# Separate due times for the first two batches' own work in a two-layer graph network kernel

## The chip, the cores and the metric

One core of one Trainium2 chip. The time is the device time of one execution, in microseconds (us); lower is better. TensorE is PE in the profile, VectorE is DVE, ScalarE is ACT, GpSimd is POOL, SyncE is SP.

## The reference

16 batches of 1024 nodes with 256 features, and an adjacency matrix of 1024 x 1024 for each. Layer 0 is masked attention with 8 heads of 32, a projection of (normed heads, features) and a residual; layer 1 is two graph attentions one after the other, a residual, and a feed-forward of width 1024. Cut to what matters:

```python
# layer 0
q, k, v = heads(x @ Wq), heads(x @ Wk), heads(x @ Wv)
e = einsum('whqd,whkd->whqk', q, k)
e = where(e >= 0, e, ALPHA * e)
attn = softmax(where(adj[:, None] > 0, e, NEG), axis=-1)
h = merge_heads(einsum('whqk,whkd->whqd', attn, v))
out = layernorm(concatenate([layernorm(h), x], -1) @ Wffn.T)
x = out + x
# layer 1
def gat(h, W, a):
    Wh = h @ W
    e = leaky_relu(Wh @ a[:256] + swap(Wh @ a[256:]), ALPHA)
    return softmax(where(adj > 0, e, NEG), axis=1) @ Wh
h = layernorm(x + gat(gat(x, W1, a1), W2, a2))
out = layernorm(h + relu(h @ w_ff1 + b_ff1) @ w_ff2 + b_ff2)
```

## The kernel before

The program is written once for all batches, and the order of its instructions is worked out when it is built. Each piece of work is a Python generator (a "thread") that tells a planner, `Order`, what it is about to do: which engine and for how long (`on`), that it waits for an event, takes or gives a buffer, or starts another thread with an aim, a due time on the planner's clock. `Order.run` asks of every active thread when its next operation could start. Among those that can start within `WINDOW` (300 ns) of the earliest, it takes the one with the lowest aim:

```python
first = min(c[0][0] for c in could)
(t, engine, cost), th = min((c for c in could if c[0][0] <= first + self.WINDOW),
                            key=lambda c: (c[1]["aim"], c[1]["no"]))
```

The thread then emits the instruction. So the planner's clock and costs give only an order: on the chip every engine, and every queue that issues DMAs, goes through its own list in that order and waits for what it needs. DVE and POOL operations that are marked `shared` exclude each other in the plan (`port`); where the chosen one is of the one engine and a shared one of the other could begin at least 100 ns sooner, that one goes first. A free choice between two engines (`evacuate`, `weights` of batch 0) is made by the planner too.

Each batch has these stages, all under the names of the code:
- `project(b)`: `x_pair` loads x (256 KB a DMA, issued by ACT) and transposes it on PE (L347); `make_mask` and `mask_part` load the adjacency (DMA issued by ACT, L393), turn it into -1 and 0 in fp8 on DVE (L399), transpose it on PE (L409) and copy it (L413); `project_qk` and `qk_part` make q and k (L461), split them in two halves that sum to the fp32 value (L464, L466) and store both halves to DRAM on SP's queue (L470); `project_v` and `v_part` make v (L490).
- `load_stacks`: reads the halves of a head's q and k back on SP's queue (L545) into one of two pairs of buffers.
- `all_scores`: per head, 8 tiles of 128 x 1024 scores on PE (L578); `weights`: leaky ReLU on ACT and DVE (L596, L594, L598), exp on ACT (L601), the mask's product on POOL (L605).
- `all_values`: weights times v on PE (L627), `after_head`: transposed (L653) and divided (L658, L660).
- `rest(b)`, begun when the last values of b are planned: `rows_pair` (norms, L729 and L732, x1, L761), the first graph attention (`first_half` L797 to L801; `attend`, eight tiles of DVE work L814 and L817; `second_rows` L851), the second (`attend` again; `normed_pair` L876), and `feed_forward` (`hidden` L916, then L944), four pairs of row tiles each.

The projections of batch b + 1 are started when the scores of batch b begin, and `rest(b)` goes on beside the tiles of batch b + 1 and, with its feed-forward, of b + 2. `begin[b]` is the planner's time when b's scores begin. `SLOT` is 253 us of the planner's clock, and every aim is a share of it, from the table `AIM`: for `project(b + 1)` counted from `begin[b]`, for `rest(b)` from its own start, for `feed_forward` from the end of its pair's norm. A name ending in `_step` is what is added from one piece to the next. Batch 0 is projected with a start of -SLOT, so that its aims are the same shares less one.

Tiles are due at equal steps after `begin[b]`, and may be planned at most `lead` steps ahead of their due time. The pace of a batch is a share of SLOT:

```python
def pace(b):
    return PACE * {0: AIM["fast0"], 1: AIM["fast1"], B - 1: AIM["fast15"]}.get(b, 1.0)
...
                    due = t0 + (h * NT + t) / 2 * pace(b)
                    yield aim(due, AIM["lead"] * PACE)
```

Of the kernel before, what the change touches and what calls it, by code (L numbers as in the profile page):

```python
# [185 lines left out]
def wait(event):  # L186
    return "wait", event
# [14 lines left out]
def start(thread, aim):  # L202
    return "start", (thread, aim)
# [21 lines left out]
def unshifted_path(  # L225
# [9 lines left out]
    B, N, D = x.shape  # L235
# [14 lines left out]
    SLOT = 253e3  # L250
    PACE = SLOT / (H * NT // 2)


    AIM = dict(mask0=0.6, x=0.818, x_step=0, mask=0.747, mask_step=0.0264, qk0=0.614, qk1=0.898, qk_step=0.0231, v0=0.832,
               v1=0.974, v_step=0.0591, rows=-0.244, rows_step=0.0408, first0=0.12, first1=0.252,
               graph0=-0.009, graph1=0.21, graph_step=0, second=0.355, second_step=0.0335, normed=0.78,
               normed_step=0.026, ff_wait=(None, 0, 1, 0), ff=(0.532, -0.011, 0.487, 0.497), ff_step=0.0386,
               fast0=0.4, fast1=0.85, fast15=0.832, lead=3.15)

    const = ctx.enter_context(tc.tile_pool(name="const", bufs=1))  # L260
    sb = ctx.enter_context(tc.tile_pool(name="sb", bufs=1))
# [3 lines left out]
    bufs = dict(misc=3, scores=2, acc=1, p=5, stacks=2, stage=2, adj=2, adjb=2, pair=18,  # L265
                xT=2, v=2, mask=2, hn=1, w8=2, big=1, job=1)
    work = Order(**bufs)

    def misc(dtype=FT):
        return psum.tile([P, HALF], dtype, tag="misc", name="ps_m", bufs=bufs["misc"])  # L270
# [148 lines left out]
    def make_mask(b, t0):  # L419
        yield take("mask")  # L420
        masks[b] = buf([P, NT * N], "mask", "mask", F8)
        parts = [(t, (kh,)) for kh in range(NH) for t in range(NT)] if b == 0 else [(t, (0, 1)) for t in range(NT)]
        for n, (t, halves) in enumerate(parts):
            yield start(mask_part(b, t, halves), t0 + (AIM["mask" if b else "mask0"] + AIM["mask_step"] * n) * SLOT)

    def mask_of(b, t):

# [49 lines left out]
    def project_qk(b, g, t0):  # L477
        scratch[b, g] = dram.tile([2, P, 2, N], FT, name="qk_halves")
        for o in range(2):
            for nh in range(NH):  # L480
                yield start(qk_part(b, g, o, nh), t0 + (2 * o + nh) * AIM["qk_step"] * SLOT)

    def v_part(b, g, u):
        yield wait(("xT", b, u))
# [18 lines left out]
    def project_v(b, g, t0):  # L503
        yield take("v")
        v = buf([P, NT, G * VW + 31], "v", "v")
        vs[b, g] = v
        yield on(POOL=500)
        nc.gpsimd.memset(v[:, :, G * VW:], 0.0)
        nc.gpsimd.memset(v[:, :, :G * VW].rearrange("p t (h c) -> p t h c", c=VW)[:, :, :, DH:], -1.0)
        for u in range(NP):  # L510
            yield start(v_part(b, g, u), t0 + AIM["v_step"] * u * SLOT)

    def project(b, t0):
        yield take("xT")
        xTs[b] = buf([P, DC, N], "xT", "xT")
        for u in range(NP):
            yield start(x_pair(b, u), t0 + (AIM["x"] + AIM["x_step"] * u if b else 0.0) * SLOT)
        yield start(make_mask(b, t0), t0 + (0.5 if b else 0.0) * SLOT)
        for g in range(H // G):
            yield start(project_qk(b, g, t0 + AIM[("qk0", "qk1")[g]] * SLOT), t0)  # L520
            yield start(project_v(b, g, t0 + AIM[("v0", "v1")[g]] * SLOT), t0 + (0.8, 1.0)[g] * SLOT)

    def load_stacks():

# [300 lines left out]
    def attention(b, s, rows, at):  # L825

        yield take("w8")
        firsts[b, s] = buf([P, 2, N], "w8", "first")
        for nh in range(NH):
            yield start(first_half(b, s, nh), at(AIM[("first0", "first1")[s]]))  # L830
        for t in range(NT):
            yield wait(("row", b, s, t))
        second = small.tile([P, NT], FT, name="second", bufs=2)
        yield on(ACT=220)
        nc.scalar.activation(second, scores_of(b, s)[:, :, 1], AF.Exp, scale=1.0 - ALPHA)
        sums = small.tile([P, NT], FT, name="sums", bufs=2)
        yield take("big")
        big = buf([P, NT, N], "big", "att")
        yield fire(("graph", b, s))
        for j in range(NT):  # L840
            yield start(attend(b, s, big, rows, j, second, sums), at(AIM[("graph0", "graph1")[s]] + AIM["graph_step"] * j))
        for j in range(NT):
            yield wait(("att", b, s, j))
        yield give("w8")
        return big
# [19 lines left out]
    def normed_pair(b, u, big, y2):  # L865

        tiles = (2 * u, 2 * u + 1)
        yield wait(("x1", b, u))
        x1 = x1s.pop((b, u))
        yield take("misc")  # L870
        pa = misc()
        for i, t in enumerate(tiles):
            for half in range(2):
                yield on(PE=1720)
                for j in range(half * NT // 2, (half + 1) * NT // 2):
                    nc.tensor.matmul(pa[:, i * D:(i + 1) * D], big[:, j, t * P:(t + 1) * P], y2[:, j, :D],  # L876
                                     start=(j == 0), stop=False)
            yield on(PE=430)
            as_rows(pa, i, x1, i)
        yield fire(("weighed", b, u))  # L880
        yield give("pair")
        y, rows, srcs = yield from taken_out(pa, "y")
        mv, rs = yield from stats(srcs)
        yield from normalized(rows, srcs, mv, rs)
        yield take("pair")
        rT = buf([P, DC, 2 * P], "pair", "rT")
        yield take("misc")
        pt = misc()
        yield on(PE=450)
        transposes(pt, rows)  # L890
        yield give("pair")
        for dc in range(DC):
            yield from by_columns(rT[:, dc, :], pt[:, dc * 2 * P:(dc + 1) * 2 * P], k["gl1c"][:, dc:dc + 1],
                                  k["bl1c"][:, dc:dc + 1])
        yield give("misc")

        if b + 1 < B and AIM["ff_wait"][u] is not None:
            yield wait(("graph", b + 1, AIM["ff_wait"][u]))
        yield start(feed_forward(b, u, rT), work.now + (AIM["ff"][u] if b + 1 < B else 0.04 * u) * SLOT)

    def as_rows(pa, i, srcT, t):

# [25 lines left out]
        yield fire(done + (hp,))  # L928

    def feed_forward(b, u, rT):  # L930
        due = work.now + (AIM["ff"][u] if b + 1 < B else 0.04 * u) * SLOT
        yield take("job")
        hid = {}
        for hp in range(HC // 2):
            yield start(hidden(hid, rT, hp, ("hid", b, u)), due + AIM["ff_step"] * hp * SLOT)
        for hp in range(HC // 2):
            yield wait(("hid", b, u, hp))
        yield take("misc")
        pa = misc()
        for i in range(2):  # L940
            for half in range(2):
                yield on(PE=1720)
                for hc in range(half * HC // 2, (half + 1) * HC // 2):
                    nc.tensor.matmul(pa[:, i * D:(i + 1) * D], hid[hc // 2][:, hc % 2, i * P:(i + 1) * P], wf2[:, hc, :],  # L944
                                     start=(hc == 0), stop=False)
            yield on(PE=430)
            as_rows(pa, i, rT, i)
        for _ in range(HC // 2 + 1):
            yield give("pair")
        yield give("job")  # L950
        y, rows, srcs = yield from taken_out(pa, "z")
        mv, rs = yield from stats(srcs)
        for i, (row, src) in enumerate(zip(rows, srcs)):
            yield on(DVE=490, shared=True)
            nc.vector.scalar_tensor_tensor(row, src, mv[:, i, 0:1], k["gl2"], op0=OP.subtract, op1=OP.mult)
            yield on(DVE=490, shared=True)
            nc.vector.scalar_tensor_tensor(row, row, rs[:, i:i + 1], k["bl2"], op0=OP.mult, op1=OP.add)
        yield load()
        nc.sync.dma_start(out[b, 2 * u * P:2 * (u + 1) * P, :].rearrange("(p i) d -> p i d", p=P), y)
        yield give("pair")  # L960
        yield fire(("out", b, u))
# [6 lines left out]
    def rest(b):  # L968
# [3 lines left out]
        def at(share):  # L972
            return t0 + share * SLOT
# [6 lines left out]
        for q in range(NH):  # L980
            yield start(head_stats(b, q), at(0))
        for u in range(NP):
            yield start(rows_pair(b, u), at(AIM["rows"] + AIM["rows_step"] * u))
        for u in range(NP):
            yield wait(("hn used", b, u))
        yield give("hn")
# [2 lines left out]
        yield take("w8")  # L989
        y2 = buf([P, NT, YW], "w8", "y2")  # L990
        for i in range(NT):
            yield start(second_rows(b, big, y1, y2, i), at(AIM["second"] + AIM["second_step"] * i))
        for i in range(NT):
            yield wait(("row", b, 1, i))
        yield give("big")
        yield give("w8")
        for u in range(2):
            yield start(fetch_x1(b, u), at(AIM["normed"]))
        big = yield from attention(b, 1, y2, at)
        yield give("mask")  # L1000
        yield start(count(b), at(1.0))
        for u in range(NP):
            yield start(normed_pair(b, u, big, y2), at(AIM["normed"] + AIM["normed_step"] * u))
        for u in range(NP):
            yield wait(("weighed", b, u))
            if u + 2 < NP:
                yield start(fetch_x1(b, u + 2), at(AIM["normed"]))
        yield give("big")
        yield give("w8")

# [409 lines left out]
```

## Time and profile before

| | |
|---|---|
| median of 3 runs | 4531.88 us (4531.49 to 4532.59) |
| profiled execution | 4533.91 us |
| its span, first to last instruction | 4532.1 us |
| granted TensorE clock, mean | 0.985 |
| busy: PE, DVE, ACT, POOL | 4352.1, 3338.5, 2888.7, 2469.0 us |
| first L578 of batches 0 to 5 | 44, 214, 493, 790, 1068, 1339 us |
| last L578 of batches 0 and 1 | 212, 467 us |
| `attend` of batch 0 (L814) | 279 to 320, 397 to 440 us |
| L851 and L876 of batch 0 | 319 to 381, 441 to 493 us |
| first L916 | 496 us |

Durations that are used: L605 2.19 us, L598 1.21, L601 1.06, L596 1.02, all on 128 x 1024.

The page cuts the span in 40 slices of 113 us and gives busy shares in tenths. An answer by windows gives, for each stretch, its length, and per engine the busy time and the number of instructions, then the granted PE clock, the DMA engines' busy share and GB/s. An answer on waits gives who waited for whom, the sum in us, how often, and the longest.

### The profile page before, as it was taken

What the parts mean: (1) busy time and instruction counts of PE and PEld (TensorE: products, weight loads), DVE (VectorE), ACT (ScalarE), POOL (GpSimd) and SP (SyncE); (2) the same over time, 40 slices, a digit from 0 to 9 for tenths busy, and PEclk for the clock granted to TensorE, in tenths of its full rate; (3) what the DMA queues carried; (4) which work ended last, traced back from release to release, by engine and by line L of the source; (5) the groups of instructions that cost most, each with busy time, mean ns of one, the idle gap of its engine ahead of it and who ended that gap; (6) DMA issues with size and microseconds to landing.
All of it is one profiled execution on the core that took longest, in us unless ns stands there. A gap on an engine that the chain in (4) does not pass through costs nothing.

```text
span 4532.1 us, 57096 instructions
## 1 busy us (share of the span) xinstructions
PE 4352.1 (96%) x20299; PEld 2889.7 (64%) x20299; DVE 3338.5 (74%) x5265; ACT 2888.7 (64%) x4012; POOL 2469.0 (54%) x1544
## 2 busy tenths in 40 slices
PE   7888999999999999999999999999999999999998
PEld 3354756666666676666767666676666667666587
DVE  6876678877787777768777777787768777776754
ACT  5656565566666666676666666666666676666631
POOL 4856465455565545655565565556655564565610
PEclk8989999999999999999999999999999999999999
DMA  6422223132232312323132232322323232232100
GB/s 181 116 65 68 73 61 96 54 84 76 62 98 63 105 56 76 94 59 110 57 88 73 59 100 70 101 66 72 85 66 100 63 93 62 69 92 54 26 22 20
DMA packets 156208, 343.57 MB, mean 76 GB/s; under 512 B 21750, under 2 KB 24332, under 8 KB 155916
## 3 DMA queue, kind: packets, MB, share of 16 engines
q1 hardware_dynamic: 109836, 255.93, 20.2%
q10 hardware_dynamic: 46080, 83.91, 6.2%
q8 instruction: 164, 2.69, 0.3%
q14 instruction: 128, 1.05, 0.1%
HBM read 239.09 MB, written 100.66 MB: 75 GB/s over the span
## 4 chain that ended last, share of the span: by engine, by line
PE 68%; DVE 19%; POOL 5%; issue 4%; ACT 3%; DMA 0%; SPq 0%; ACTq 0%; POOLq 0%; DVEq 0%
PE ps_a L627 15%; PE ps_s L578 9%; PE ps_m L876 8%; PE ps_m L851 7%; PE ps_m L916 7%; PE ps_m L944 6%; DVE att L817 5%; DVE att L814 5%; POOL p L605 4%; DVE p L598 4%; PE ps_m L461 3%; PE ps_m L761 2%; PE ps_m L729 2%; PE ps_m L732 2%; PE ps_m L347 2%
## 5 line engine op out<-in xcount | busy, mean ns | idle before, releaser
L605 POOL TENSOR_TENSOR p<-p,mask 128x1024 f32<-128x1024 f32 x1024 | 2228.3, 2193 | 1588.5 <-ACT p L601 1492.6
L598 DVE TENSOR_TENSOR p<-p,ps_s 128x1024 f32<-128x1024 f32 x1024 | 1210.8, 1213 | 407.9 <-ACT p L596 406.4
L601 ACT ACTIVATE p<-p 128x1024 f32<-128x1024 f32 x1024 | 1081.4, 1058 | 385.8 <-DVE p L598 363.3
L596 ACT ACTIVATE p<-ps_s 128x1024 f32<-128x1024 f32 x996 | 976.6, 1024 | 202.8 <-PE ps_s L578 185.7
L627 PE MATMUL ps_a<-p,v 128*33 128x512 f32 (+1 forms) x4096 | 999.1, 605 | 28.6 <-POOL p L605 27.6
L578 PE MATMUL ps_s<-qs,ks 128*128 128x512 f32 x2048 | 640.4, 432 | 54.5 <-DVE p L598 51.3
L578 PEld LDWEIGHTS ps_s<-qs,ks 128*128 128x128 f32 x2048 | 353.7, 192 | 358.2 <-DVE p L598 118.3
L627 PEld LDWEIGHTS ps_a<-p,v 128*33 128x33 f32 (+1 forms) x4096 | 198.5, 113 | 532.5 <-issue 399.7
L876 PE MATMUL ps_m<-y,att 128*128 128x256 f32 x2048 | 484.3, 383 | 13.7 <-ACT v L499 11.0
L944 PE MATMUL ps_m<-wf,hid 128*128 128x256 f32 x2048 | 478.0, 383 | 9.1 <-ACT xT L305 8.7
L851 PE MATMUL ps_m<-y,att 128*128 128x258 f32 x2048 | 474.4, 382 | 5.6 <-ACT hid L925 3.7
L916 PE MATMUL ps_m<-rT,wf 128*128 128x256 f32 x2048 | 473.6, 380 | 4.2 <-DVE hid L922 1.4
L944 PEld LDWEIGHTS ps_m<-wf,hid 128*128 128x128 f32 x2048 | 382.3, 191 | 77.8 <-issue 14.0
L851 PEld LDWEIGHTS ps_m<-y,att 128*128 128x128 f32 x2048 | 386.7, 190 | 70.4 <-ACT hid L925 4.4
L876 PEld LDWEIGHTS ps_m<-y,att 128*128 128x128 f32 x2048 | 378.8, 191 | 80.1 <-ACT v L499 13.1
L916 PEld LDWEIGHTS ps_m<-rT,wf 128*128 128x128 f32 x2048 | 377.3, 190 | 54.9 <-PE ps_m L461 1.7
L814 DVE SCALAR_TENSOR_TENSOR att<-first,second 128x1024 f32<-128x1024 f32 x256 | 354.0, 1383 | 73.1 <-ACT first L801 73.1
L817 DVE SCALAR_TENSOR_TENSOR att<-mask,att 128x1024 f32<-128x1024 fp8e4 x256 | 363.3, 1419 | 8.7
L822 ACT ACTIVATE y<-y,check 128x258 f32<-128x258 f32 x256 | 130.8, 511 | 321.7 <-DVE check L820 297.9
L330 POOL TENSOR_SCALAR rs<-mv 128x2 f32<-128x2 f32 (+1 forms) x224 | 59.0, 264 | 443.7 <-DVE mv L327 443.6
L399 DVE TENSOR_SCALAR adj_b<-adj_i 128x512 fp8e4<-128x512 int32 x256 | 244.3, 997 | 25.5 <-DMA adj_i<-in_adj_dram 19.3
L925 ACT ACTIVATE hid<-ps_m,columns 128x256 f32<-128x256 f32 x373 | 159.5, 471 | 118.5 <-PE ps_m L916 92.8
(103 smaller groups left out, 4266.9 us busy)
## 6 DMA issues: line engine op xcount, KB each, us to landing
adj_i<-in_adj_dram ACTq DMA_DIRECT2D x256, 256.0 KB, 3.5
qs<-qk_halves SPq DMA_DIRECT2D x256, 256.0 KB, 4.0
ks<-qk_halves SPq DMA_DIRECT2D x256, 256.0 KB, 4.9
qk_halves<-high SPq DMA_DIRECT2D x128, 256.0 KB, 2.5
qk_halves<-low SPq DMA_DIRECT2D x128, 256.0 KB, 3.8
xr<-in_x_dram ACTq DMA_DIRECT2D x64, 256.0 KB, 2.9
x_kept<-x SPq DMA_DIRECT2D x64, 256.0 KB, 2.0
x<-x_kept SPq DMA_DIRECT2D x64, 256.0 KB, 5.3
```

What stands on the lines that cost most here:

```text
L578: nc.tensor.matmul(ps[i][:, cols], kk[:, (t + i) * P:(t + i + 1) * P], q[:, cols], start=True, stop=True)
L596: nc.scalar.activation(p, ps, AF.Copy, scale=ALPHA)
L598: nc.vector.tensor_tensor(p, p, ps, op=OP.max)
L601: nc.scalar.activation(p, p, AF.Exp)
L605: nc.gpsimd.tensor_tensor(p, p, mask_of(b, t), op=OP.mult)
L627: nc.tensor.matmul(acc[nh * 64:nh * 64 + m, :], v[:, t, c:c + m], p[:, nh * HALF:(nh + 1) * HALF], start=(t == 0), stop=(t == NT - 1))
L814: nc.vector.scalar_tensor_tensor(e, first[:, 0, :], second[:, j:j + 1], first[:, 1, :], op0=OP.mult, op1=OP.max)
L817: nc.vector.scalar_tensor_tensor(e, mask_of(b, j), -1.0, e, op0=OP.mult, op1=OP.mult, accum_out=sums[:, j:j + 1])
L851: nc.tensor.matmul(pa[:, cols:cols + width], big[:, j, i * P:(i + 1) * P], rows[:, j, :width], start=(j == 0), stop=(j == NT - 1))
L876: nc.tensor.matmul(pa[:, i * D:(i + 1) * D], big[:, j, t * P:(t + 1) * P], y2[:, j, :D], start=(j == 0), stop=False)
L916: nc.tensor.matmul(pa[:, i * 2 * P:(i + 1) * 2 * P], wf1[:, dc, hc * P:(hc + 1) * P], rT[:, dc, :], start=(dc == 0), stop=(dc == DC - 1))
L944: nc.tensor.matmul(pa[:, i * D:(i + 1) * D], hid[hc // 2][:, hc % 2, i * P:(i + 1) * P], wf2[:, hc, :], start=(hc == 0), stop=False)
```

## The change

A second table, `EARLY`, stands beside `AIM`. A function `share` picks between them by batch, and every use of the named aims in `project`, `rest` and what they start goes through it. The work of `rest(b)` and `feed_forward(b)` takes `EARLY` for b = 0 and 1. Projections take it by b - 1: for batches 0, 1 and 2. Three values of `AIM` itself change: `mask0`, `fast0` and `fast1`. No instruction, buffer or transfer is added or removed. For b of 2 and more the old aims stand.

```diff
-    AIM = dict(mask0=0.6, x=0.818, x_step=0, mask=0.747, mask_step=0.0264, qk0=0.614, qk1=0.898, qk_step=0.0231, v0=0.832,
-               v1=0.974, v_step=0.0591, rows=-0.244, rows_step=0.0408, first0=0.12, first1=0.252,
-               graph0=-0.009, graph1=0.21, graph_step=0, second=0.355, second_step=0.0335, normed=0.78,
-               normed_step=0.026, ff_wait=(None, 0, 1, 0), ff=(0.532, -0.011, 0.487, 0.497), ff_step=0.0386,
-               fast0=0.4, fast1=0.85, fast15=0.832, lead=3.15)
+    AIM = dict(mask0=0.759, x=0.818, x_step=0, mask=0.747, mask_step=0.0264, qk0=0.614, qk1=0.898,
+               qk_step=0.0231, v0=0.832, v1=0.974, v_step=0.0591, rows=-0.244, rows_step=0.0408, first0=0.12,
+               first1=0.252, graph0=-0.009, graph1=0.21, graph_step=0, second=0.355, second_step=0.0335,
+               normed=0.78, normed_step=0.026, ff_wait=(None, 0, 1, 0), ff=(0.532, -0.011, 0.487, 0.497),
+               ff_step=0.0386, fast0=0.425, fast1=0.938, fast15=0.832, lead=3.15)
+
+    EARLY = dict(x=0.87, x_step=0.005, mask=0.747, mask_step=0.0296, qk0=0.692, qk1=0.909, qk_step=0.0345,
+                 v0=0.774, v1=1.001, v_step=0.0568, rows=-0.139, rows_step=0.0071, first0=0.082, first1=-0.169,
+                 graph0=-0.195, graph1=-0.027, graph_step=0, second=0.302, second_step=0.0335, normed=0.781,
+                 normed_step=0.02, ff_wait=(None, 0, 1, 0), ff=(0.633, -0.001, 0.488, 0.497), ff_step=0.0386)
...
+
+    def share(b, name):
+        return (EARLY if b < 2 else AIM)[name]
...
-            yield start(mask_part(b, t, halves), t0 + (AIM["mask" if b else "mask0"] + AIM["mask_step"] * n) * SLOT)
+            yield start(mask_part(b, t, halves),
+                        t0 + ((share(b - 1, "mask") if b else AIM["mask0"]) + share(b - 1, "mask_step") * n) * SLOT)
...
-            yield start(x_pair(b, u), t0 + (AIM["x"] + AIM["x_step"] * u if b else 0.0) * SLOT)
+            yield start(x_pair(b, u), t0 + (share(b - 1, "x") + share(b - 1, "x_step") * u if b else 0.0) * SLOT)
...
-            yield start(attend(b, s, big, rows, j, second, sums), at(AIM[("graph0", "graph1")[s]] + AIM["graph_step"] * j))
+            yield start(attend(b, s, big, rows, j, second, sums),
+                        at(share(b, ("graph0", "graph1")[s]) + share(b, "graph_step") * j))
```

The other uses change in the same way, `AIM[name]` to `share(b - 1, name)` in `project_qk`, `project_v` and `project`, and to `share(b, name)` in `attention`, `rest`, `normed_pair` and `feed_forward`.

More of the change, by code (lines that the diff above doesn't have):

```diff
@@ L480, in project_qk @@
             for nh in range(NH):
-                yield start(qk_part(b, g, o, nh), t0 + (2 * o + nh) * AIM["qk_step"] * SLOT)
+                yield start(qk_part(b, g, o, nh), t0 + (2 * o + nh) * share(b - 1, "qk_step") * SLOT)
     def v_part(b, g, u):
@@ L510, in project_v @@
         for u in range(NP):
-            yield start(v_part(b, g, u), t0 + AIM["v_step"] * u * SLOT)
+            yield start(v_part(b, g, u), t0 + share(b - 1, "v_step") * u * SLOT)
     def project(b, t0):
@@ L516, in project @@
         for u in range(NP):
-            yield start(x_pair(b, u), t0 + (AIM["x"] + AIM["x_step"] * u if b else 0.0) * SLOT)
+            yield start(x_pair(b, u), t0 + (share(b - 1, "x") + share(b - 1, "x_step") * u if b else 0.0) * SLOT)
         yield start(make_mask(b, t0), t0 + (0.5 if b else 0.0) * SLOT)
         for g in range(H // G):
-            yield start(project_qk(b, g, t0 + AIM[("qk0", "qk1")[g]] * SLOT), t0)
-            yield start(project_v(b, g, t0 + AIM[("v0", "v1")[g]] * SLOT), t0 + (0.8, 1.0)[g] * SLOT)
+            yield start(project_qk(b, g, t0 + share(b - 1, ("qk0", "qk1")[g]) * SLOT), t0)
+            yield start(project_v(b, g, t0 + share(b - 1, ("v0", "v1")[g]) * SLOT), t0 + (0.8, 1.0)[g] * SLOT)
     def load_stacks():
@@ L829, in attention @@
         for nh in range(NH):
-            yield start(first_half(b, s, nh), at(AIM[("first0", "first1")[s]]))
+            yield start(first_half(b, s, nh), at(share(b, ("first0", "first1")[s])))
         for t in range(NT):
@@ L895, in normed_pair @@
         yield give("misc")
-        if b + 1 < B and AIM["ff_wait"][u] is not None:
-            yield wait(("graph", b + 1, AIM["ff_wait"][u]))
-        yield start(feed_forward(b, u, rT), work.now + (AIM["ff"][u] if b + 1 < B else 0.04 * u) * SLOT)
+        if b + 1 < B and share(b, "ff_wait")[u] is not None:
+            yield wait(("graph", b + 1, share(b, "ff_wait")[u]))
+        yield start(feed_forward(b, u, rT), work.now + (share(b, "ff")[u] if b + 1 < B else 0.04 * u) * SLOT)
     def as_rows(pa, i, srcT, t):
@@ L930, in feed_forward @@
     def feed_forward(b, u, rT):
-        due = work.now + (AIM["ff"][u] if b + 1 < B else 0.04 * u) * SLOT
+        due = work.now + (share(b, "ff")[u] if b + 1 < B else 0.04 * u) * SLOT
         yield take("job")
@@ L934, in feed_forward @@
         for hp in range(HC // 2):
-            yield start(hidden(hid, rT, hp, ("hid", b, u)), due + AIM["ff_step"] * hp * SLOT)
+            yield start(hidden(hid, rT, hp, ("hid", b, u)), due + share(b, "ff_step") * hp * SLOT)
         for hp in range(HC // 2):
@@ L982, in rest @@
         for u in range(NP):
-            yield start(rows_pair(b, u), at(AIM["rows"] + AIM["rows_step"] * u))
+            yield start(rows_pair(b, u), at(share(b, "rows") + share(b, "rows_step") * u))
         for u in range(NP):
@@ L991, in rest @@
         for i in range(NT):
-            yield start(second_rows(b, big, y1, y2, i), at(AIM["second"] + AIM["second_step"] * i))
+            yield start(second_rows(b, big, y1, y2, i), at(share(b, "second") + share(b, "second_step") * i))
         for i in range(NT):
@@ L997, in rest @@
         for u in range(2):
-            yield start(fetch_x1(b, u), at(AIM["normed"]))
+            yield start(fetch_x1(b, u), at(share(b, "normed")))
         big = yield from attention(b, 1, y2, at)
@@ L1002, in rest @@
         for u in range(NP):
-            yield start(normed_pair(b, u, big, y2), at(AIM["normed"] + AIM["normed_step"] * u))
+            yield start(normed_pair(b, u, big, y2), at(share(b, "normed") + share(b, "normed_step") * u))
         for u in range(NP):
@@ L1006, in rest @@
             if u + 2 < NP:
-                yield start(fetch_x1(b, u + 2), at(AIM["normed"]))
+                yield start(fetch_x1(b, u + 2), at(share(b, "normed")))
         yield give("big")
```

## The prediction

> **What bounds the kernel now.** I read the page first, for where the time is lost at all. The chain that ended last is TensorE (PE) for most of the span; of the slices, only the first ones hold an idle or a slow PE.
>
> ```profile
> PE   7888999999999999999999999999999999999998
> PEclk8989999999999999999999999999999999999999
> PE 68%; DVE 19%; POOL 5%; issue 4%; ACT 3%; DMA 0%; SPq 0%; ACTq 0%; POOLq 0%; DVEq 0%
> ```
>
> The first line is PE's busy share, the second its granted clock, in tenths. Next I cut the span where a batch's first score matmul (L578) starts: 44, 214, 493, 790, 1068, 1339 us, and asked for busy times by stretch (length, PE, PEld, DVE, ACT, POOL, clock).
>
> ```profile
> 44.00:214.00 170.00, 141.51 (x557) 58.58 (x557) 144.53 (x140) 115.38 (x135) 132.92 (x64) 0.91 0.40 112
> 214.00:493.00 279.00, 241.38 (x1015) 142.44 (x1012) 193.40 (x276) 166.97 (x217) 163.59 (x90) 0.89 0.28 79
> 493.00:790.00 297.00, 274.31 (x1255) 180.69 (x1253) 223.56 (x338) 180.97 (x250) 163.99 (x93) 0.97 0.26 73
> 790.00:1068.00 278.00, 268.74 (x1272) 178.35 (x1268) 214.28 (x335) 180.55 (x247) 152.08 (x97) 1.00 0.27 78
> 1068.00:1339.00 271.00, 267.25 (x1267) 178.45 (x1265) 204.34 (x325) 182.37 (x253) 152.91 (x97) 1.00 0.27 78
> ```
>
> A later slot takes 271 us with PE busy for 267: it loses 4 us. I count a stretch's loss as its length less PE's busy time, plus (1 - clock) times its length. Batch 0's slot loses 28.5 + 15.3 = 44, batch 1's 37.6 + 30.7 = 68, batch 2's 22.7 + 8.9 = 32, batch 3's 9. That is 153 us, about 137 above the 4 us of a good slot. Nothing else can be won by a change to the order of the first batches; work only moved in time is paid elsewhere.
>
> Where in batch 1's slot? Cut into 50 us, the two bad stretches lie on either side of a full one:
>
> ```profile
> 300.00:350.00 50.00, 43.69 (x154) 23.67 (x155) 35.63 (x43) 33.70 (x43) 31.66 (x14) 0.83 0.21 62
> 350.00:400.00 50.00, 49.88 (x225) 28.16 (x223) 25.82 (x31) 39.66 (x49) 36.58 (x20) 1.00 0.25 65
> 400.00:450.00 50.00, 33.37 (x106) 14.97 (x106) 47.05 (x55) 27.45 (x35) 29.59 (x11) 0.80 0.29 80
> ```
>
> The last loses 16.6 + 10 = 27 us, with DVE busy for 47 of 50. It is the second graph attention of batch 0: eight `attend` tiles on DVE, between the scores of batch 1. L817 alone, over the two attentions of batch 0 and one of batch 4:
>
> ```profile
> 278.00:322.00 44.00, 18.95 (x15) 0.77 0.25 72
> 396.00:446.00 50.00, 20.88 (x16) 0.80 0.25 71
> 1398.00:1421.00 23.00, 9.86 (x16) 1.00 0.15 46
> ```
>
> Eight tiles take 44 and 50 us here, 23 later. Later POOL stands still meanwhile (1.4 us busy of 23, against 29.6 of 50). PE's own waits from 44 to 790 us say the same:
>
> ```profile
> PE ps_s L578 <- DVE p L598: 41.0, 28, 4.1
> PE ps_a L627 <- POOL p L605: 18.6, 23, 2.0
> ```
>
> PE is idle because softmax tiles come too slowly from DVE and POOL, not for want of data from DMA.
>
> [...] L817 (mask and att, both in SBUF) agrees: 3.03 us beside L605, 1.22 alone, and two L605 then take 6.16 us for 4.24. [...] granted clocks of 0.5 last 3.4 us or multiples, 17.1 us at 427. [...]
>
> **The change part by part.** No instruction is added or removed, and no wait. `Order.run` takes, of the operations that can start within 300 ns of the earliest, the one with the lowest aim; every engine and queue then runs in that fixed order. So a part is worth something only where it changes who is lowest. I write aims in us after a batch's begin (SLOT is 253 us; rest(0) starts 7 us after begin[1]: last L627 of batch 0 at 221, first L578 of batch 1 at 214).
>
> *Start.* mask0 goes from -101 to -61 us, qk0 of batch 0 from -98 to -78, v0 from -42 to -57. The first q and k parts now precede the masks, and the second group comes behind more of v. L545 issued the first stack at 34.1 us, right after the last L470 of group 1 at 33.7; group 0's last part was issued at 23.3, and lands 3.8 later (page): 27. SP's order costs up to 7 us. But the plan puts the loads behind writes by its own due times, and I see no reason for all eight writes to change places. Masks moved back (their loads on ACT's queue, 0.33 us each, too) can delay the first L605, now at 48.8, by as much. -7 to +6; I take -2.
>
> *Batch 0's tiles.* fast0 0.4 to 0.425 moves the last due time from 101 to 107 us, while they need 170: they are always late, lowest, and limited by DVE (144.5 of 170) and POOL. x, qk, v and mask aims of batch 1 (189 us and more, or 175) stay fillers behind them. v_step, qk_step and mask_step do no more. 0, -4 to +4.
>
> *Work of batch 0 beside batch 1's tiles.* Before, tile n is due at 3.36n us (0.85 x 253 / 64), now at 3.71n. rows at -55 to -24 becomes -28 to -23; first0, graph0, first1, graph1 go to lower aims still. Before, graph1 stood at 60, while at 397 us tiles about 44 (148 us) compete. They were lower than every competing tile already, so lowering them flips nothing: what lets POOL between two `attend` tiles is the planner's rule for the shared port, which isn't changed. I cost these edits at 0, -10 to +5. Two comparisons do flip:
> - `second_rows` i: 97 + 8.5i becomes 83 + 8.5i. Tiles up to 29 preceded i = 0, now up to 22: 7 tiles. A tile is 1.6 us of PE (39.3 / 64 for L578 + 62.4 / 64 for L627, in a later slot). 11 us of PE leave the full stretch 350:400 for 400:450, which has 27 to fill. The tiles still need 1.21 us of DVE and 2.16 of POOL each there, so I take half: -5.
> - `normed_pair` u: 204 + 6.6u against tiles up to 61, now 205 + 5.1u against up to 55: 6 tiles, 10 us of PE. The L876 group, 441 to 493, ends up to 10 us earlier, and the feed-forward (first L916 at 496) with it. The delayed tiles run beside it: the stretch from 500 loses 4.4 + 1.5 us. -3.
> Sum -8, from -25 to +15: +15 if the tiles' delay is not refilled.
>
> *Batch 2's slot.* second of batch 1 is 13.4 us lower against tiles at 3.95n: 3.4 tiles, 5 us of PE into stretches that lose 32 in all: -3. ff[0] 0.532 to 0.633 holds the first feed-forward (32 x 2 x 0.23 = 15 us of PE) 26 us longer as filler, towards 600:750, where PE still waits: -2. x, qk0 and mask of batch 2 come 13 to 20 us later; their stack was in time (last tile of batch 1 at 467, batch 2 at 493 with PE full of L876 between): 0, up to +8 if that cover goes, as then the stack comes late next. Sum -5, -15 to +10.
>
> Later slots keep their aims: 0. Total -2 + 0 - 8 - 5 = -15, against the profiled execution's 4533.9 (span 4532.1): 4518.9. It lay 2.0 above the median of the runs, 4531.9: **4517**.
>
> **Rivals.**
> *A larger gain.* Lower aims and later tiles do make the attentions exclusive, as in batch 4. Then four blocks (44, 50, 45, 46 us) need 23 each[...]. PE lost 15 + 27 us around the first two and about 17 around the others; two thirds of 59 gone is -40: 4492. For it: the later slots show this state with graph aims higher than these. Against: they have feed-forward to keep PE from new tiles; batch 1 has none.
> *Nothing.* Dependences, not aims, set the order of the first 800 us: 4532. For it: most aims were already lowest. Against: the two flips.
> *Slower.* The later pace takes tiles from PE when nothing else can run. The last tile of batch 1 is due 22 us later and the feed-forward is held 26 us longer. If graph products and pairs are done before the tiles, POOL stands still and PE meets the end of batch 1 with tiles alone, limited as in batch 0's slot: 2.66 us a tile (170 / 64) for 1.6 of work. Over 13 overtaken tiles that is +14, with half clock for as long +20: 4552. It decides if the first L578 of batch 2 comes later than 493 plus what the first feed-forward got ahead.
>
> **How the numbers follow.** A measurement can tell 0.2%, 9 us, from no change. The -15 case has 0.41 (of it 0.05 under 9 us), the larger gain 0.20, nothing 0.12, slower 0.27 (of it 0.03 under 9 us). Faster 0.56, same 0.20, slower 0.24. Taken alone the likeliest case reaches from 4500 to 4526. For 8 in 10 the range takes in most of the larger gain and of the slower case: 4488 to 4556.
>
> **What would show it.** Right: `attend` of batch 0 still 40 us or more each; the last L851 of batch 0 some 10 us before 381; L876 ended before 490; batch 1's slot loses 55 to 62 instead of 68. The larger gain: L817 in it near 1.2 us. Slower: POOL idle in 440:500 beyond today's, batch 2 begun after 505. Wrong altogether: a gain or loss in slots after 1068, or in the drain after 4304, where no aim changes.

## The result, and the profile after

The changed kernel takes 4502.8 us (median of 4 runs, 4495.8 to 4507.5) against 4531.7: a ratio of 0.9935, 95% interval 0.9917 to 0.9952. That is 29 us less, on the side forecast (4517, range 4488 to 4556), and nearly twice the 15 us of the sum. The profiled execution took 4506.1 us, with a span of 4504.3.

The slices of the page, PE's busy share and granted clock as before:

```profile
PE   7888999999999999999999999999999999999998
PEclk9989999999999999999999999999999999999999
```

At this grain almost nothing has moved. Cut again where each batch's first score matmul starts (now 45, 206, 483, 763, 1036, 1306 us), the busy times by stretch are these (length, PE, PEld, DVE, ACT, POOL, clock):

```profile
44.00:206.00 162.00, 137.91 (x557) 57.19 (x557) 142.75 (x142) 112.88 (x134) 134.07 (x65) 0.92 0.48 136
206.00:483.00 277.00, 241.84 (x1057) 145.60 (x1053) 197.81 (x289) 171.94 (x227) 163.87 (x89) 0.91 0.26 73
483.00:763.00 280.00, 266.33 (x1236) 175.20 (x1234) 202.21 (x326) 175.77 (x241) 164.50 (x95) 0.98 0.27 77
763.00:1036.00 273.00, 265.21 (x1249) 175.06 (x1248) 209.38 (x331) 179.79 (x247) 152.63 (x97) 1.00 0.27 78
1036.00:1306.00 270.00, 266.26 (x1264) 178.33 (x1263) 204.36 (x325) 182.34 (x253) 151.92 (x97) 1.00 0.27 78
```

With the prediction's measure (length less PE's busy time, plus the clock's part) the first four slots lose 37, 60, 19 and 8 us, in place of 44, 68, 32 and 9. The sum is 29 us less with the clock in hundredths. With the clock unrounded and the cuts exact it is 33 us less (154 to 121), and these four slots are shorter by as much (1024.1 to 991.0 us, table below). From batch 4 on a slot takes 270.3 to 271.6 us in both kernels. Outside the four slots the profiled execution gives 5 us back: three slots of 271.6 where before had one, 488.9 for 487.0 us from batch 15's first L578 to the end, 0.7 at the start. PE's waits from 44 to 763 us answer to those shown of before:

```profile
PE ps_s L587 <- DVE p L607: 23.5, 22, 2.6
PE ps_a L636 <- POOL p L614: 18.7, 19, 2.1
```

(L587, L607, L636, L614 are L578, L598, L627, L605 of before.) The scores wait 17.5 us less for the buffers that DVE frees, the values as long as before for POOL.

### The profile page after: what moved, and what is told of

It is laid out like the page before. It is cut to its first block, busy times and chain, and to the rows that moved or that the text cites. A ratio compares the mean times of both kernels' runs of the same rounds, so it can differ in the third digit from the quotient of the medians.

```text
span 4504.3 us, 57113 instructions
## 1 busy us (share of the span) xinstructions
PE 4341.5 (96%) x20299; PEld 2887.0 (64%) x20299; DVE 3312.6 (74%) x5262; ACT 2886.2 (64%) x4015; POOL 2471.3 (55%) x1544
## 4 chain that ended last, share of the span: by engine, by line
PE 70%; DVE 18%; issue 4%; POOL 4%; ACT 3%; DMA 0%; POOLq 0%; ACTq 0%; SPq 0%; DVEq 0%
PE ps_a L636 16%; PE ps_s L587 9%; PE ps_m L886 9%; PE ps_m L861 7%; PE ps_m L926 7%; PE ps_m L954 6%; DVE att L826 5%; DVE att L823 5%; POOL p L614 4%; DVE p L607 3%; PE ps_m L470 3%; PE ps_m L770 2%; PE ps_m L738 2%; PE ps_m L741 2%; PE ps_m L355 2%
## 5 line engine op out<-in xcount | busy, mean ns | idle before, releaser
L614 POOL TENSOR_TENSOR p<-p,mask 128x1024 f32<-128x1024 f32 x1024 | 2231.4, 2196 | 1585.2 <-ACT p L610 1484.6
L607 DVE TENSOR_TENSOR p<-p,ps_s 128x1024 f32<-128x1024 f32 x1024 | 1211.4, 1214 | 412.2 <-ACT p L605 410.8
L605 ACT ACTIVATE p<-ps_s 128x1024 f32<-128x1024 f32 x993 | 973.0, 1025 | 196.8 <-PE ps_s L587 176.9
L636 PE MATMUL ps_a<-p,v 128*33 128x512 f32 (+1 forms) x4096 | 999.2, 606 | 29.1 <-POOL p L614 27.9
L587 PE MATMUL ps_s<-qs,ks 128*128 128x512 f32 x2048 | 636.3, 430 | 37.0 <-DVE p L607 33.7
L587 PEld LDWEIGHTS ps_s<-qs,ks 128*128 128x128 f32 x2048 | 351.4, 191 | 339.5 <-DVE p L607 98.8
L636 PEld LDWEIGHTS ps_a<-p,v 128*33 128x33 f32 (+1 forms) x4096 | 199.7, 114 | 535.4 <-issue 409.4
L823 DVE SCALAR_TENSOR_TENSOR att<-first,second 128x1024 f32<-128x1024 f32 x256 | 354.7, 1385 | 73.1 <-ACT first L810 73.1
L826 DVE SCALAR_TENSOR_TENSOR att<-mask,att 128x1024 f32<-128x1024 fp8e4 x256 | 354.1, 1383 | 8.7
L407 DVE TENSOR_SCALAR adj_b<-adj_i 128x512 fp8e4<-128x512 int32 x256 | 229.2, 938 | 21.7 <-DMA adj_i<-in_adj_dram 12.7
```

The source lines that it names most:

```text
L587: nc.tensor.matmul(ps[i][:, cols], kk[:, (t + i) * P:(t + i + 1) * P], q[:, cols], start=True, stop=True)
L605: nc.scalar.activation(p, ps, AF.Copy, scale=ALPHA)
L607: nc.vector.tensor_tensor(p, p, ps, op=OP.max)
L614: nc.gpsimd.tensor_tensor(p, p, mask_of(b, t), op=OP.mult)
L636: nc.tensor.matmul(acc[nh * 64:nh * 64 + m, :], v[:, t, c:c + m], p[:, nh * HALF:(nh + 1) * HALF], start=(t == 0), stop=(t == NT - 1))
L823: nc.vector.scalar_tensor_tensor(e, first[:, 0, :], second[:, j:j + 1], first[:, 1, :], op0=OP.mult, op1=OP.max)
```

## The experiments

All are built from the changed kernel's text with `share` in place. "Before with" means that `EARLY` is `dict(AIM)` and all numbers are the old ones but those named; such a text without a named number gives before's order. One table first, as the argument lies in it: the length of each slot in us, from the first L578 of a batch to that of the next, the median time, and two columns more. "Lost" is the prediction's measure over slots 0 to 2 together, with the clock unrounded. A slot is also shorter when less of PE's work falls into it (slots 0 to 2 hold 2821 PE instructions in before, 2843 in the changed kernel, 2785 in p4 and p8), so the loss tells more than the length. "Repeats" is the first slot from which PE's instructions in the trace are, line by line and in the same order, those of every later slot up to 14.

| kernel | slot 0 | 1 | 2 | 3 | 4 | 5 | 6 | time | lost | repeats |
|---|---|---|---|---|---|---|---|---|---|---|
| before | 170.3 | 278.6 | 297.4 | 277.8 | 270.7 | 270.6 | 270.3 | 4531.7 | 145.3 | 4 |
| changed | 161.6 | 276.5 | 280.3 | 272.6 | 270.7 | 270.7 | 270.3 | 4502.8 | 113.6 | 4 |
| p1: pace alone | 172.4 | 271.8 | 291.5 | 294.7 | 289.1 | 300.5 | 279.9 | 4633.7 | 142.5 | 10 |
| p2: projections alone | 162.5 | 270.3 | 293.2 | 279.9 | 272.5 | 295.3 | 296.9 | 4574.7 | 121.2 | 8 |
| p3: rest alone | 170.4 | 282.6 | 285.0 | 293.8 | 294.7 | 288.6 | 294.1 | 4794.0 | 143.3 | never |
| p4: changed, old pace | 163.9 | 259.9 | 301.8 | 279.1 | 308.3 | 285.4 | 295.3 | 4703.7 | 141.5 | never |
| p5: q and k alone | 166.4 | 273.6 | 298.1 | 277.8 | 270.6 | 270.6 | 271.8 | 4522.1 | 138.1 | 4 |
| p6: v alone | 169.1 | 271.6 | 297.2 | 277.8 | 270.7 | 270.3 | 270.4 | 4528.0 | 136.2 | 4 |
| p7: changed, old rest | 159.5 | 276.6 | 277.9 | 279.0 | 271.6 | 270.6 | 270.6 | 4504.0 | 116.8 | 4 |
| p8: mask_step alone | 169.0 | 270.7 | 286.9 | 285.6 | 292.9 | 290.7 | 290.9 | 4794.6 | 132.3 | never |
| p9: p8, and pace of batch 2 | 168.3 | 267.3 | 281.9 | 286.5 | 277.5 | 271.7 | 270.9 | 4523.6 | 120.0 | 5 |
| p10: changed, old second | 159.3 | 269.5 | 278.9 | 299.4 | 282.5 | 277.5 | 271.7 | 4534.2 | 113.8 | 6 |
| p11: changed, old first and graph | 161.6 | 265.4 | 288.7 | 278.5 | 309.2 | 280.7 | 280.4 | 4556.9 | 128.5 | 7 |

All kernels that come to repeat do so with one and the same order of 1264 PE instructions a slot. Times of single slots scatter: PE's order is the same in p8 and p9 up to batch 2, and slot 1 took 270.7 and 267.3 us.

### The three groups of the change, each alone (p1, p2, p3), and all without the pace (p4)

```diff
# p1, before with
-               fast0=0.4, fast1=0.85
+               fast0=0.425, fast1=0.938
# p2, before with
-    AIM = dict(mask0=0.6,
+    AIM = dict(mask0=0.759,
+    EARLY = dict(AIM, x=0.87, x_step=0.005, mask_step=0.0296, qk0=0.692, qk1=0.909, qk_step=0.0345,
+                 v0=0.774, v1=1.001, v_step=0.0568)
# p3, before with
+    EARLY = dict(AIM, rows=-0.139, rows_step=0.0071, first0=0.082, first1=-0.169, graph0=-0.195, graph1=-0.027,
+                 second=0.302, normed=0.781, normed_step=0.02, ff=(0.633, -0.001, 0.488, 0.497))
# p4, changed with
-               fast0=0.425, fast1=0.938
+               fast0=0.4, fast1=0.85
```

What was expected of p1:

> The kernel before with only fast0 = 0.425 and fast1 = 0.938; all other aims as before. Theory A (the gain comes from the tiles of batch 1 being due later than the graph products of batch 0): 4531.7 less about 5, so 4524 to 4530, with batch 0's slot (before 170.3 us, after 161.6) unchanged. Theory B (the pace of batch 0 is what shortens batch 0's slot): the slot falls to 162 to 165 us and the time to about 4520. Theory C (it is the projections' aims): no change, 4529 to 4534.

Measured: 4633.7, ratio 1.0225 (1.0208 to 1.0242). None of the theories. Slots 0 to 2 together are 11 us shorter than before's (3 us by the loss); slots 3 to 6 are 75 us longer, although no aim of theirs was touched.

> The kernel before with only mask0 and the aims of the projections of batches 0 to 2 (x, masks, q and k, v) from the new table; pace and rest as before. Theory A: 4527 to 4532, slot of batch 0 near 170. Theory B: the same. Theory C (earlier v and later masks and q, k of batch 1 fit better beside batch 0's tiles): the slot falls to 162 to 165 us, the time to about 4521.

Measured: 4574.7, ratio 1.0094 (1.0077 to 1.0110). On slot 0 theory C is right, 162.5 us; the time is the other way. Slots 0 to 2 give 20 us (24 by the loss), slots 3 to 6 take 55.

> The kernel before with only the aims of the rest of batches 0 and 1 (rows, first, graph, second, normed, feed-forward) from the new table. Theory A: slots of batches 1 and 2 (before 278.6 and 297.4 us) lose 5 to 12 us together, 4519 to 4527; batch 0's slot cannot change, since no rest runs in it. Theory C: 4529 to 4534. Rival D (the three groups work only together): slower than before, 4535 to 4550.

Measured: 4794.0, ratio 1.0570 (1.0553 to 1.0588): rival D by sign, far beyond its size. None of the slots 1 to 14 of this kernel takes less than 282 us.

> The changed kernel with the old pace (fast0 = 0.4, fast1 = 0.85). Theory A: half of the gain of batches 1 and 2 is gone, 4508 to 4515. Theory B: batch 0's slot is back at 170 and the time at 4511 or more. Theory C: 4500 to 4506, as with the new pace. Rival D: 4525 or more.

Measured: 4703.7, ratio 1.0372 (1.0354 to 1.0389), as D had it (4525 or more). Again the first three slots are shorter than before's (725.6 against 746.3), but with 36 PE instructions fewer, and they lose nearly as much.

So the effects of the groups don't add: +101, +42 and +261 us alone (beside before's 4532.6 on the same chip), -29 together. And most of the loss of each lies in slots whose aims nobody changed (of p3's aims only the feed-forward's of batch 1 reach beyond slot 2). From this came theory E. A slot whose plan begins in the same state as the one before it gets the same order, so the order can repeat itself from slot to slot; it does so in before and after from batch 4 on, at 270.6 us. The early aims act in two ways: some microseconds in slots 0 to 2, and when, or whether, that repetition is reached. The last column of the table bears this out: kernels that repeat from slot 4 take 4503 to 4532 us, from 5, 6 and 7 on 4524, 4534 and 4557, from 8 and 10 on 4575 and 4634, and those that never do 4704 to 4795.

### Parts that keep the repetition (p5, p6, p7), and one that breaks it (p8)

```diff
# p5, before with
+    EARLY = dict(AIM, qk0=0.692, qk1=0.909, qk_step=0.0345)
# p6, before with
+    EARLY = dict(AIM, v0=0.774, v1=1.001, v_step=0.0568)
# p7, changed with (all of the rest's aims old)
+    EARLY = dict(AIM, x=0.87, x_step=0.005, mask_step=0.0296, qk0=0.692, qk1=0.909, qk_step=0.0345,
+                 v0=0.774, v1=1.001, v_step=0.0568)
# p8, before with
+    EARLY = dict(AIM, mask_step=0.0296)
```

> The kernel before with only qk0, qk1 and qk_step of the first three projections from the new table (0.692, 0.909, 0.0345). Theory E (the early aims act in two ways: they shorten the slots of batches 0 to 2 by some us each, and they decide from which slot on the order repeats itself at 270.6 us a slot; out of that order a slot takes 280 to 300): in this kernel's list the order after the first slots is the one of before, so the time falls by what the first slots give, 4521 to 4528; if it is the q and k parts that shorten batch 0's slot, that slot is 162 to 165 us. Rival F (slots are shortened by the v parts, made at 135 us instead of 169): slot 170, time 4529 to 4534.

Measured: 4522.1, ratio 0.9977 (0.9967 to 0.9986). The time is as E has it. Slot 0 took 166.4, 4 us less than before but not the 162 to 165 of the whole group.

> The kernel before with only v0, v1 and v_step of the first three projections from the new table (0.774, 1.001, 0.0568). Theory E: 4529 to 4534, slot of batch 0 at 168 to 171. Rival F: slot 162 to 165, time 4521 to 4527.

Measured: 4528.0, ratio 0.9993 (0.9985 to 1.0001): no difference that these runs tell. Slot 0 took 169.1, so rival F falls: v alone isn't it.

> The changed kernel with the old aims for the rest of batches 0 and 1 (rows, first, graph, second, normed, feed-forward): the new pace and the new projections together. Each of these two alone was slower than before. Theory E: together they enter the repeating order at batch 3 or 4 as the changed kernel does, 4500 to 4515. Theory A of the first runs (the overtaking by second and normed is the gain): 4515 to 4525. Rival D, sharpened (all three groups are needed): 4540 or more.

Measured: 4504.0, ratio 0.9934 (0.9921 to 0.9948), the same as the changed kernel within both intervals, and as E had it. Pace and projections, each slower alone, carry the whole gain together; the new aims of the rest add nothing to it. The projections alone (p2) already bring the loss of slots 0 to 2 from 145 to 121 us, p7's is 117; with the pace added the order repeats from slot 4, not 8. This kernel also decides on the prediction's first rival. L817 (L823 here) over batch 0's two attentions in p7:

```profile
263.00:286.00 23.00, 9.86 (x16) 0.77 0.17 57
351.00:374.00 23.00, 9.86 (x16) 0.64 0.03 11
```

and over the same two in the changed kernel (L826 there):

```profile
265.00:309.00 44.00, 17.74 (x15) 0.73 0.26 78
377.00:424.00 47.00, 20.87 (x16) 0.89 0.20 62
```

In p7 the `attend` tiles take 22 us a block, with the 9.86 us for L817 of before's batch 4, where POOL was busy for 1.4 of 23 us; in the changed kernel they take 44 and 46 us, with POOL busy for 25.8 of 44 and 27.7 of 47. Batch 1's two blocks in p7 are exclusive too (21 and 22 us, 9.86 each for L817). Meanwhile PE is busy for 13.8 of the first 23 us and 3.4 of the second, with the clock at 0.77 and 0.64. Slots 1 and 2 of p7:

```profile
204.00:481.00 277.00, 233.26 (x1029) 141.26 (x1025) 190.43 (x287) 169.72 (x222) 150.21 (x90) 0.90 0.26 71
481.00:759.00 278.00, 268.63 (x1257) 176.34 (x1256) 197.79 (x325) 182.33 (x251) 147.85 (x94) 0.99 0.27 78
```

They lose 71 and 12 us, where the changed kernel's lose 60 and 19. What exclusive attentions save on DVE in slot 1 is lost there again on PE, and the time is the same.

> The kernel before with one number changed: mask_step 0.0264 to 0.0296 for the first three projections, at most 5.7 us later for the last mask part. Theory E: the first three slots together change by less than 10 us either way, but the order does not come to repeat itself, and the later slots take 280 to 300 us: 4650 or more. The way of reckoning of the prediction (each aim costs what it moves): within 10 us of 4532.

Measured: 4794.6, ratio 1.0580 (1.0564 to 1.0596). One number, moved by 0.0032 of a slot, costs nine times what the whole change gains. Its first three slots are 20 us shorter together than before's (13 by the loss), beyond the 10 that E allowed. Then every slot but one takes 285 to 314. Three of them by stretch, in p8:

```profile
1059.00:1352.00 293.00, 272.21 (x1258) 177.86 (x1256) 212.52 (x335) 177.79 (x242) 157.32 (x96) 0.98 0.25 70
1352.00:1643.00 291.00, 274.47 (x1271) 182.77 (x1270) 212.96 (x330) 183.09 (x252) 160.29 (x97) 0.98 0.27 75
1643.00:1934.00 291.00, 274.94 (x1273) 182.40 (x1273) 220.16 (x340) 178.56 (x242) 161.90 (x97) 0.99 0.26 74
```

Nearly the same number of PE instructions as in a good slot (1267), but 16 to 21 us of PE idle instead of 4, and a clock of 0.98 to 0.99. L817 in the same stretches of p8:

```profile
1059.00:1352.00 293.00, 32.67 (x32) 0.98 0.25 70
1352.00:1643.00 291.00, 27.10 (x32) 0.98 0.27 75
1643.00:1934.00 291.00, 30.77 (x32) 0.99 0.26 74
```

and in good slots of before:

```profile
1068.00:1339.00 271.00, 19.72 (x32) 1.00 0.27 78
1339.00:1610.00 271.00, 19.72 (x32) 1.00 0.28 78
1610.00:1881.00 271.00, 19.73 (x32) 1.00 0.27 78
```

The same to a hundredth in all three: this is what the repetition looks like in a trace. In p8 an attention of most slots falls among the tiles again, and DVE spends 7 to 13 us more on the 16 L817 of that one; the other is exclusive, as both are in before. That is a part of the 20 us; the rest isn't divided further here.

### Breaking and mending (p9, p10, p11)

```diff
# p9, p8 with
-        return PACE * {0: AIM["fast0"], 1: AIM["fast1"], B - 1: AIM["fast15"]}.get(b, 1.0)
+        return PACE * {0: AIM["fast0"], 1: AIM["fast1"], 2: 0.99, B - 1: AIM["fast15"]}.get(b, 1.0)
# p10, changed with
-                 second=0.302
+                 second=0.355
# p11, changed with
-                 first0=0.082, first1=-0.169, graph0=-0.195, graph1=-0.027
+                 first0=0.12, first1=0.252, graph0=-0.009, graph1=0.21
```

> The kernel with mask_step alone changed, and one number more: batch 2's tiles are due at 0.99 of the pace of the later batches. Theory E: the first three slots (batches -1 to 1) keep the order of the kernel with mask_step alone, and batch 1's slot ends within 2 us of its 486.8; but now the order comes to repeat itself from batch 4 or 5 on at 270.6 us a slot, so the time falls from 4795 to 4510 to 4530. Rival G (mask parts that come later burden every slot of the first batches, and what they set back stays): 4750 or more.

Measured: 4523.6, ratio 0.9985 (0.9978 to 0.9991). The later mask parts are all still there, and 271 us of loss are gone with one number more, the pace of batch 2. The order repeats from slot 5, as E had it. Rival G falls. Batch 1's slot ended at 483.1, 3.7 us before p8's, where at most 2 was expected. Since PE's order is the same in both up to there, this is the scatter of single executions; four kernels with the same aims in slot 0 differ there by 2.4 us (159.2 to 161.6).

> The changed kernel with second back at 0.355 for batches 0 and 1, all else new. The prediction's first flip (products of the first attention overtake 7 tiles, -5 us there, -3 in batch 2's slot): slots 0 to 2 together 8 us longer, 4511. Theory E: slots 0 to 2 within 6 us of the changed kernel's, but the repeating order is reached later, by slots of 280 to 300 us between; in the list it seems to come at batch 5 or 6 instead of 4, so 4525 to 4560.

Measured: 4534.2, ratio 1.0010 (1.0001 to 1.0018). Slots 0 to 2 are 10.7 us shorter than the changed kernel's, not 8 longer, but 34 PE instructions have moved out of them, and they lose the same (113.8 and 113.6). So undoing what the prediction held for its first flip costs nothing there. Slots 3 to 6 are 46.8 us longer. E was right on the time and the slot of the repetition (6); its bound of 6 us on the first slots was too narrow for their length.

> The changed kernel with first0, first1, graph0 and graph1 back at their old values for batches 0 and 1. The prediction (lowering what is already lowest flips nothing, 0): 4498 to 4507. Theory E: the order differs from slot 1 on and comes to repeat itself only at batch 7, so 4535 to 4600, with the loss after batch 3.

Measured: 4556.9, ratio 1.0061 (1.0045 to 1.0076). The edits that the prediction costed at 0 hold 54 us here. Slots 0 to 2 are 2.7 us shorter with 50 PE instructions fewer, and lose 15 us more; slots 3 to 6 are 64.5 us longer. E had the time, and the slot of the repetition (7).

Two further parts were not run, because nothing of them reaches the chip: with `rows` and `rows_step` old, and with `ff` old, the changed kernel's lists of instructions are the same on every engine and queue, entry for entry.

### The other end (p12)

If aims of their own pay at the start, the last batches may want them too; there the slot of batch 15 and the drain lose 21.8 and 13.2 us of PE (length less its instructions, each at its mean share of PE in good slots). A third table for the last two batches (entries that equal `AIM`'s left out):

```diff
+    LATE = dict(AIM, mask=0.7067, qk0=0.6465, qk_step=0.0248, v0=0.7765, v1=0.8279, rows=-0.178, rows_step=0.0504,
+                second=0.2469, second_step=0.0358, normed_step=0.0307)
-        return (EARLY if b < 2 else AIM)[name]
+        return (EARLY if b < 2 else AIM if b < B - 2 else LATE)[name]
...
-    (share(b, "ff")[u] if b + 1 < B else 0.04 * u)
+    (share(b, "ff")[u] if b + 1 < B else 0.069 * u)
```

> The changed kernel with a third table for the last two batches' own work (second 0.355 to 0.247, rows -0.244 to -0.178, masks, q, k and v of the last projection, the last feed-forwards' spacing 0.04 to 0.069). Up to batch 14 the order is the changed kernel's. The last slot and the drain lose 21.8 + 13.2 us of PE there; if a third of what is above the 4 us of a good slot can be had, the time is 4493 to 4499 against 4502.8, no difference if the drain is bound by its own chain (the last batch's attentions and norms).

Measured: 4497.6 (4494.8 to 4499.9), ratio to before 0.9925 (0.9912 to 0.9939); the changed kernel's was 0.9935 (0.9917 to 0.9952). The time is in the range expected, but a gain over the changed kernel isn't shown. The intervals overlap, and the profiles don't place one at the end: from the first L578 of batch 14 to the end p12 takes 753.5 us and the changed kernel 760.5, but p9 and p11, with the old aims there, take 754.0 and 753.4.

## Why the prediction was right, and by which wrong steps

**The place was right.** All of the gain lies in the first four slots, which the prediction had named as the only place where time could be won. They are 33 us shorter, and its measure of loss falls by as much (154 to 121). In the first three slots of before, idle time of PE and lost clock together came to 1.4 to 1.8 times the idle time (28.5 + 15.3, 37.6 + 30.7, 22.7 + 8.9). That the one brings the other isn't shown. *Start* came out within its range: the first L578 at 44.8 us for 44.1.

**The likeliest case's signs came true without its reasons.** `attend` of batch 0 takes 44 and 46 us, its last L851 ends at 368, L876 at 469, slot 1 loses 60. Each was foretold. But p2, which has neither the pace nor the aims of the rest from which they were derived, shows all four (41 and 45 us, 361, 477, 59), and is 42 us slower than before; p7 has the changed kernel's time with attentions of 22 us and 71 lost in slot 1. And of the 13 and 24 us by which L851 and L876 end earlier, 8 are those of slot 0, which the prediction had put at 0. Signs that other causes give as well prove no mechanism; that the sum pointed the right way was in part luck.

**"0, -4 to +4" for batch 0's tiles failed:** -8.7 us. Called fillers, the projections' pieces were taken as free. They are not free on DVE: L399 (L407 after), the masks' conversion, took in slot 0 of before

```profile
44.00:214.00 170.00, 24.96 (x16) 0.91 0.40 112
```

and of the changed kernel

```profile
45.00:206.00 161.00, 19.64 (x16) 0.92 0.48 134
```

for the same 16 instructions: 1.56 us each in the mean, then 1.23. That is not the whole cause. DVE also did three more leaky ReLUs (31 of L594's kind for 28, 3.7 us), so its busy time in the slot fell by 1.8 us only (144.5 to 142.8); the other 7 us are idle time of DVE, and what ended that isn't taken apart here. p2 shows the group of aims that does it (162.5), p5 half of it (166.4). `v` and `mask_step` alone give 1 us each (169.1, 169.0), no more than the scatter; `x` and `mask0` alone were not tried.

**"-8" for the rest of batch 0 has the right size (slot 1 lost 8 less) from the wrong terms.** The first flip hardly took place. Counted in the traces, the eight groups of L851 had 20, 24, 26, 28, 32, 34, 36 and 40 tiles of batch 1 ahead of them, and have 20, 22, 24, 28, 30, 32, 36 and 38 in the changed kernel: 0 to 2 fewer, where 7 were reckoned. p2 and p10, with the old `second`, have the changed kernel's counts to the tile. The first L851 starts within 7 us of the end of the attention that feeds it in every kernel here (before: 319 and 322, changed: 312 and 310), so it seems to go by `attend` and not by its own aim. The second flip is real: L876's four groups had 56, 62, 64 and 64 tiles ahead, now 52, 56, 58 and 60. But p2 loses 59 us in slot 1 with 52, 58, 64 and 64, so the size doesn't rest on it. The -2 for `ff` was for an edit that changes no instruction.

**"0" for lowering first and graph failed (p11).** Undone, slots 0 to 2 lose 15 us more, and batch 0's attentions take 22 us each in place of 44 and 46: the edit does flip something. The argument looked only at the pairs of work that met in before's order. With the rest of the change these pieces can meet others; which ones isn't shown.

**"-5" for batch 2's slot was mis-sized:** 32 to 19, so -13. The new aims of batch 1's rest, from which it was reckoned, are not needed: p7 has the old ones and loses 12 there. The masks of batch 2 are due 0 to 6 us later, not 13 to 20 as the prediction says (`mask` itself stays), and p8 shows what that little can do.

**"Later slots keep their aims: 0" is the step whose failure could have been dear.** For the changed kernel it came true. As a rule it is false. In slots 3 to 6, p1, p2 and p8 take 55 to 75 us more than before, and p4, p10 and p11 47 to 84 us more than the changed kernel, and in those slots none of their aims differs from what they are compared with. This also shows what was wrong with adding parts. The terms of such a sum have no values of their own: the groups gave +101, +42 and +261 alone. The rival on the slower side, +20 from starved tiles (14 of idle time, and 6 as the author's estimate for half clock as long as that; before's slot 0 lost 15.3 by the clock beside 28.5 idle), named too small a price and the wrong place; the danger was an order that comes to repeat itself late or never. The slots from 3 on that were out of it in p1 to p4 and p8 to p11 took 2 to 44 us more than 270.6, 19 in the mean.

**The larger gain, exclusive attentions, is refuted.** p7 has all four blocks at 21 to 22 us, as that rival described, and is 28 us faster than before, no more than the changed kernel, which has none; p3 has those of batch 0 and is 261 us slower. L817 was slower where POOL was at work: 16 of them took 9.86 us in p7's blocks and in before's batch 4, there with POOL busy for 1.4 of 23 us, and 20.87 in the changed kernel's second block, with POOL busy for 27.7 of 47. Why isn't shown, and it doesn't price an order.

What remains open is which event in slots 2 and 3 decides whether the repetition is reached. p9 shows that a shift of 1% in batch 2's due times can decide it, not why. Pace and rest together, without the projections, were not run.

## What to carry to other kernels

Where a planner fixes the order from due times, read a trace by slots, and find from which slot on they repeat: a change to the first slots is worth what it gives there plus what it does to the arrival at that order, and the second can be ten times the first. Don't add up the prices of single aims; run the parts, and run them together. And when a stretch is foretold to improve by a certain mechanism, name a sign that only this mechanism gives.

## What the runs showed of the hardware

Slots in the repeated order take 270.3 to 270.9 us across kernels and batches in 88 of 104 cases and 271.6 to 271.8 in the others, and L817 in three of before's agrees to 0.01. Of the 16 conversions of L399 in slot 0 of before, the four that took 0.41 or 0.42 us had L605 beside them for none to 59% of that time, the twelve of 0.85 to 2.37 us for 88% or more; in the changed kernel one of 0.42 us had it beside for the whole. That the engines keep the planned order shows in the traces of before and of the changed kernel: from slot 5 to 14, semaphore entries left out, every slot has PE's 1264 matmuls, DVE's 325 entries, ACT's 273, POOL's 96 and SP's 60 in one order, line by line. Whole executions of one program agree less well: the changed kernel's four runs span 11.7 us, and go with the granted clock (4506.1 and 4507.5 us at 0.987, 4499.4 at 0.989, 4495.8 at 0.990). Before's first four spanned 1.1, but 22 later runs of it on another chip spanned 11.5 (4525.7 to 4537.2).
